# A four-layer graph network: the decoder's first expert tiles ahead of the last block's routing, joined with spare store buffers, node numbers loaded by POOL, and projection weights at the far end of memory

## The chip, the cores and the metric

The kernel runs on one core of a Trainium2 chip. The core has five engines with queues of their own: PE (TensorE, matmul), DVE (VectorE), ACT (ScalarE), POOL (GpSimd) and SP (SyncE, which only issues transfers). Sixteen DMA engines move data between HBM and the on-chip memories SBUF (128 partitions) and PSUM (where matmuls accumulate). DMA transfers are issued from the queue of an engine, here SP's, POOL's or ACT's, and that engine's instructions run in their order. The metric is the device time of one execution in microseconds (us).

## The reference, cut to what matters

Four layers, each a masked graph attention and a feed-forward part with residuals, over 2708 nodes of 256 features in fp32. The change touches the end of layer 1's feed-forward part and all of layer 2.

```python
# layer 1, feed-forward: one of eight experts for each node
H = gelu(xf @ W1 + b1)                                  # 2708 x 1024
probs = softmax(H @ Wg + bg); assign = argmax(probs)
for e in range(8):
    out = out + where(assign == e, probs[:, e] * (H @ Wd[e] + bd[e]), 0)

# layer 2, graph attention: dense over 2708 x 2708, masked by adj
e = where(adj > 0, leaky_relu((Wh @ a1)[:, None] + (Wh @ a2)[None, :]), NEG)
h_prime = softmax(e, axis=1) @ Wh

# layer 2, feed-forward: causal attention, then two of eight experts for each node
h = rmsnorm(x, ln1_w)
q, k, v = h @ wq.T, h @ wk.T, h @ wv.T                  # 4 heads of 64, 2 key/value heads, rope on q and k
y = softmax(causal(q @ k.T / 8)) @ v
x = x + y @ wo.T
flat = rmsnorm(x, ln2_w)
probs = softmax(flat @ router_w.T); tp, ti = top_k(probs, 2); tp = tp / sum(tp)
for e in range(8):
    hh = silu(flat @ w1[e].T) * (flat @ w3[e].T)        # hidden width 682
    out = out + weight_of(e) * (hh @ w2[e].T)
x = x + out
```

On the reference's inputs the eight experts of layer 2 hold 796, 754, 680, 588, 740, 790, 519 and 549 slots (node and choice), in tiles of 128: 7, 6, 6, 5, 6, 7, 5 and 5, together 47. After the first 2560 nodes they hold 759, 715, 636, 561, 700, 745, 485 and 519.

## The kernel before, in words

The 2708 nodes are 22 tiles of 128 (the last has 20 rows), the residual X stays in SBUF. The kernel is written for a framework that orders instructions by the order of the code and places all waits; `tc.issue_after(i)` pins what follows behind instruction i. Memory comes from pools that are used as stacks from either end; `side="right"` puts a pool at the far end. A pool's memory can be used only when what lay there before is free, and the framework makes the first writer wait for that.

**Layer 1, feed-forward (`top1_ffn`, L877).** In blocks of up to 512 nodes, F = gelu(x W1) is computed transposed, then turned back by PE (L960), copied to a buffer `hr` of [128, 512] (L961, ACT or DVE) and stored to DRAM as `hidden` (`store`, L950). For the last two blocks, which are stored late, `store` takes eight slots of `room`, three spare tiles that reuse other buffers (L1018–L1023); the second of them gets no room and uses the `hr` buffers, of which there are three. Meanwhile each node's slot with its expert is found and its number scattered to DRAM. `route.finish()` works out which expert each of the tiles of 128 slots belongs to. `load_first` (L1627, called at L1040) reads the node numbers of the first eight tiles on SP's queue, PE transposes them (L1045 on), and POOL gathers rows of `hidden` by them for the expert matmuls (y, L1110).

**Layer 2, graph attention (`gat_single` "g2", L1164).** A loop over column blocks i0 and, within, over 22 source tiles j (L1296 on): ACT makes e (L674), DVE masks it (L675), PE accumulates (acc, L1310). During it the experts' weights w2 are loaded (`Weights`, L1366), by 16 transfers from SP after a memset of POOL.

**Layer 2, attention (`attention`, L1691).** The pool `a_w` (L1732) holds ln1, wv, wk and wq, loaded on POOL's queue (L1735, L93) when the graph attention's memory is free, and scaled by ln1 in six DVE operations (L1739). `project` makes q, k and v of one of six column blocks of 512 nodes (the last has 148), beginning with the normed rows f (L108), their transposes (tp, L1759) and pv (L123). `attend` (L1793) goes over the key tiles: sc (L1817, PE), e = exp (L1830, ACT), masks on the diagonal (L1834), po (L1836, PE), and sums of e (L1842), of which every third goes to a second sum on POOL:

```python
                part = j % 3 == 2
```

At the end pd (L1848, PE) adds up the sums, yt is 1/pd times po (L1852, L1853). The last block does both pairs of heads at once (m = 2). `send` (L1857) is a generator: wo (wy, L123), residual, root mean square (Newton iteration, L313–L322), transposes, router logits (L1899), and `Routing.chunk` (L1468), which finds both choices by first maximum (L855–L861), their rank within the expert (L1497), and scatters the rows h with their numbers to slots of `hs` in DRAM (L1518, POOL). Block n−1's `send` and block n+1's `project` run between the key steps of block n, paced by `between`: 14 steps are counted for `send`. After the last block its own `send` runs alone, `weights.more()` loads w3 (eight transfers of 682 KB, SP, L1392).

**Layer 2, experts (`experts`, L1951).** Before it `route.finish()` (L1528) counts and assigns tiles to experts; then `owners` (L1569, what each tile holds and where its results go), `shares` (softmax weights of the two choices, and `Head`, the next layer's weights). Tiles 0 to 7 are the first tile of each expert, so their place in `hs` is known beforehand; later ones are read through a register (L1625). A tile s goes: f (fetched by SP, five buffers), PE transposes (tp) and ACT copies to ft (`front`), h = ft w1 and ft w3 (`hidden`, L1990, two halves of 682 columns), SiLU (L2003), `gate` on DVE (hh, L2007), six transposes pt (L2014), copies to ht (L2015 on DVE, L2016 on ACT), po = ht w2 (L2022), y (L2026) and `send`, the scatter of the results by POOL (L1648). `place(s)` (`where`, L1633) works out, in three DVE operations from f's last two columns, to which row each result goes. The loop pipelines two tiles, and in it `place(s + 2)` stands before `gate(s + 1)`:

```python
                        front(s + 2)
                        place(s + 2)
```

`through(0, route.usual)` does the 47 usual tiles; `others` (L1596) is a conditional body for more, entered when `further` says that there are more, which on these inputs it does not. Then `combine` reads the results back in layer 3.

## Time and profile before

| | |
|---|---|
| median of three executions | 2853.9 us (2853.67 to 2859.36) |
| profiled execution | 2853.26 us, span 2851.6 us |
| granted clock of TensorE | 0.955 |
| busy, share of the span | PE 92%, PEld 57%, DVE 51%, ACT 36%, POOL 13% |
| end of layer 1's stores to its first y | 1208 to 1227 us |
| last acc of layer 2 to the first pv | 1616.0 to 1628.6 us |
| last exp of attention to the first pt of the experts | 2102.1 to 2145.1 us |
| expert tiles, first pt to last | 2145.1 to 2531.2 us |

The page is one profiled execution. PEld is the loading of weights into PE, which overlaps matmuls. PEclk is the clock that PE was granted, as a share of full speed. A group reads: line, engine, operation, out<-in, shape, count, busy us and mean ns, idle time before it and what ended it. The chain of waits is the chain of work that ended last, followed back from the end to what released each step. A fp32 matmul makes several records.

### The profile page before, as it was taken

Reading aid. Unit: us, or ns where it says so; the run is one execution under the profiler, and the core shown is the slowest. Engines: PE = TensorE matmul, PEld = TensorE weight load, DVE = VectorE, ACT = ScalarE, POOL = GpSimd, SP = SyncE. Lnnn points to the kernel's source line nnn. Section 1 sums busy time; section 2 is a strip of 40 time slices with the busy share of each in tenths; the row PEclk is TensorE's granted clock in tenths of the full one; section 3 lists DMA queues with packets and bytes.
Section 4 is the critical chain, followed back from the end, with each engine's and each line's share of the span. In section 5 each row is a group of like instructions: output and inputs, shape, how many; then the busy total and the mean of one; then the engine's idle time right before and its main releaser. Section 6 shows DMA issues by size and latency. Waiting matters only on the chain.

```text
span 2851.6 us, 32365 instructions
## 1 busy us (share of the span) xinstructions
PE 2625.3 (92%) x11712; PEld 1616.6 (57%) x11712; DVE 1446.4 (51%) x3086; ACT 1040.0 (36%) x1639; POOL 381.5 (13%) x470
## 2 busy tenths in 40 slices
PE   5999989799999999888999899999969999969998
PEld 4667746563333444577788533333337777757885
DVE  7753348453777765422544456464653222245555
ACT  3344433224665653311543223233322221225453
POOL 1000012100000001143300123223331111110002
PEclk9999999797999999989999999899979999989999
DMA  8899210000000003753200100002031111041001
GB/s 295 288 299 326 97 65 1 3 5 1 1 1 1 1 3 115 169 176 128 85 1 1 34 23 18 16 0 94 16 117 32 30 30 34 28 137 62 1 1 40
DMA packets 107336, 197.67 MB, mean 69 GB/s; under 512 B 8831, under 2 KB 64361, under 8 KB 104341
## 3 DMA queue, kind: packets, MB, share of 16 engines
q1 hardware_dynamic: 89178, 147.89, 16.4%
q0 software_dynamic: 14624, 43.22, 4.6%
q10 hardware_dynamic: 3374, 4.46, 0.5%
q8 instruction: 98, 1.61, 0.2%
q14 instruction: 62, 0.50, 0.1%
HBM read 135.82 MB, written 59.71 MB: 69 GB/s over the span
## 4 chain that ended last, share of the span: by engine, by line
PE 74%; DVE 9%; issue 5%; DMA 5%; ACT 3%; POOL 3%; another core or an unknown queue 0%; ACTq 0%; SPq 0%; POOLq 0%; DVEq 0%
PE acc L1310 15%; PE acc L805 8%; PE acc L284 7%; PE den L816 4%; PE po L2022 4%; PE po L1836 3%; PE sc L1817 3%; PE score L273 3%; PE pv L123 3%; PE h L1990 3%; DMA f<-hs 2%; PE h L943 2%; PE po L123 2%; PE sc L1785 2%; PE pl L123 1%
## 5 line engine op out<-in xcount | busy, mean ns | idle before, releaser
L675 DVE SCALAR_TENSOR_TENSOR e<-e,mask 128x768 f32<-128x768 f32 (+2 forms) x264 | 411.3, 1573 | 310.2 <-ACT e L674 309.9
L674 ACT ACTIVATE e<-big_p,minus_one,ratio 128x768 f32<-128x768 f32 (+2 forms) x264 | 394.9, 1513 | 368.4 <-PE acc L1310 229.7
L1310 PE MATMUL acc<-V,e 128*128 128x257 f32 (+1 forms) x1936 | 433.5, 383 | 4.5 <-DVE e L675 4.4
L1310 PEld LDWEIGHTS acc<-V,e 128*128 128x128 f32 (+1 forms) x1936 | 352.3, 186 | 85.7 <-issue 32.1
L805 PE MATMUL acc<-e,V 128*64 128x512 f32 (+1 forms) x1056 | 244.3, 551 | 4.4 <-DVE e L675 4.4
L1990 PE MATMUL h<-w,ft 128*128 (+1 forms) x752 | 233.5, 453 | 0.5 <-ACT ft L1972 0.5
L284 PE MATMUL acc<-F,e 128*128 128x257 f32 x968 | 226.3, 384 | 3.1 <-DVE e L281 2.7
L284 PEld LDWEIGHTS acc<-F,e 128*128 128x128 f32 x968 | 173.4, 185 | 67.1 <-DVE e L281 28.5
L805 PEld LDWEIGHTS acc<-e,V 128*64 128x64 f32 x1056 | 107.5, 137 | 163.8 <-issue 131.2
L1817 PE MATMUL sc<-qt,kt 64*128 64x512 f32 (+5 forms) x568 | 177.2, 576 | 4.1 <-ACT e L1830 2.4
L1830 ACT ACTIVATE e<-sc 128x1024 f32<-128x1024 f32 (+3 forms) x120 | 99.6, 859 | 188.8 <-PE sc L1817 169.4
L1990 PEld LDWEIGHTS h<-w,ft 128*128 128x128 f32 x752 | 136.1, 191 | 56.7 <-issue 1.4
L281 DVE TENSOR_TENSOR e<-e,mask 128x512 f32<-128x512 f32 (+2 forms) x132 | 80.4, 625 | 150.3 <-ACT e L275 148.7
L1842 DVE TENSOR_TENSOR sum<-sum,e 128x1024 f32<-128x1024 f32 (+4 forms) x88 | 100.1, 1138 | 77.2 <-ACT e L1830 70.0
L275 ACT ACTIVATE e<-score 128x512 f32<-128x512 f32 (+2 forms) x132 | 69.7, 544 | 179.1 <-PE score L273 152.5
L2022 PE MATMUL po<-w,ht 114*128 (+1 forms) x564 | 129.5, 379 | 0.9 <-DVE ht L2015 0.9
L1836 PE MATMUL po<-e,V 128*64 128x512 f32 (+3 forms) x480 | 111.7, 547 | 16.8 <-ACT e L1830 8.7
L816 PE MATMUL den<-e,low 128*3 128x512 f32 (+1 forms) x1056 | 123.8, 542 | 0.3 <-DVE e L675 0.3
L2022 PEld LDWEIGHTS po<-w,ht 114*128 114x128 f32 x564 | 106.7, 189 | 22.6 <-DVE ht L2015 8.2
L1638 DVE TENSOR_SCALAR second<-f,down 128x1 f32<-128x1 f32 x47 | 9.9, 213 | 213.2 <-DMA f<-hs 213.2
L1817 PEld LDWEIGHTS sc<-qt,kt 64*128 64x128 f32 (+1 forms) x568 | 60.8, 191 | 94.1 <-issue 78.0
L273 PE MATMUL score<-QK 128*128 128x512 f32 (+2 forms) x264 | 112.1, 555 | 1.2 <-ACT e L275 0.7
(618 smaller groups left out, 3510.9 us busy)
## 6 DMA issues: line engine op xcount, KB each, us to landing
row<-in_adj SPq DMA_DIRECT2D x21, 1354.0 KB
raw<-in_adjT SPq DMA_DIRECT2D x35, 768.0 KB
hs<-zero SPq DMA_DIRECT2D x8, 2838.0 KB
hidden<-hr SPq DMA_DIRECT2D x34, 256.0 KB
wd<-in_f_wd SPq DMA_DIRECT2D x8, 1024.0 KB
kept<-mask SPq DMA_DIRECT2D x21, 338.5 KB
mask<-kept SPq DMA_DIRECT2D x21, 338.5 KB
f<-hs SPq DMA_DIRECT2D x47, 129.0 KB
```

The lines of the kernel that those rows point to most:

```text
L123: self.nc.tensor.matmul(out, lhsT[:, c, :], rhs[:, c, :], start=first and c == 0, stop=last and c == n - 1)
L273: nc.tensor.matmul(ps[:r, :iw], QK[:, 0, span(j)], QK[:, 1, i0 : i0 + iw], start=True, stop=True)
L284: nc.tensor.matmul(acc[k][:ri], e[:r, k * P : k * P + ri], F[:r, j, :], start=j == 0, stop=j == NT - 1)
L674: nc.scalar.activation(v, big_p[:, i], AF.Relu, bias=net.minus_one, scale=ratio)
L675: return nc.vector.scalar_tensor_tensor(v, v, 1.0, net.mask[:, j, i], ALU.add, ALU.mult)
L805: made = nc.tensor.matmul(acc[n][half, :iw], V[:, j, h, :], e[:, k, i0 : i0 + iw], start=j == 0, stop=j == NT - 1)
L816: made = nc.tensor.matmul(den[g : g + Q, :iw], low[:, j, h, Q - 1 - q : 2 * Q - 1 - q], e[:, k, i0 : i0 + iw], start=False, stop=j == NT - ...
L1310: nc.tensor.matmul(acc[k][:ri], e[:, k * P : k * P + ri], V[:, j, :], start=j == 0, stop=j == NT - 1)
L1817: nc.tensor.matmul(by_pairs(ps[:r, g])[:, :, o:], kt[b, span(j)], qt[b, :, o:iw], start=True, stop=True)
L1836: nc.tensor.matmul(by_pairs(po[b])[:, :, o:], V[:r, j, g, :], by_pairs(e[:r, g])[:, :, o:], start=j == 0, stop=j == last,)
L1990: last = nc.tensor.matmul(halves[s, n][:, q, :HALF], fts[s][:, c, :], weights.w13[n][:, es[s], c, q * HALF : (q + 1) * HALF], start=c == 0 ...
L2022: last = nc.tensor.matmul(po, ht[:KP, k, :], w2[:KP, es[s], k, :], start=k == 0, stop=k == KC - 1)
```

## The change

Four things are changed.

1. `store` takes its buffers from `room` for both late blocks, and `room` has a fourth spare tile (the buffers of `w1`, four more [128, 512]).
2. `load_first` issues from POOL's queue in place of SP's.
3. `a_w` lies at the far end of memory; in the changed program POOL's queue has the loads of ln1, wv, wk and wq directly after the memset of w2, early in the graph attention. The six scalings are pinned behind that loop's masked e of j = 3 in the first column block.
4. In attention's last block all sums are DVE's, the results lie in a tile `yl` of their own, and 24 steps are counted for block n−1's `send`. After it `route.cut` works out, from the counts of five blocks, where the results of the first eight tiles go (128 slots, or as many as the expert holds so far). Attention calls `mixture`, which loads the SiLU table by a small operation, fetches eight tiles at once (three from ACT's queue, five from POOL's, eight buffers instead of five), and runs the tiles with `beside`, a generator with the last block's `send`, `finish`, `owners` and `Head`, of which a step is taken at two places before the first pt and at three in every tile after it, until tile 4 takes what is left. `shares` comes after the last tile's gate, without `Head`. `place(s + 2)` stands behind `gate(s + 1)`. Since a tile was taken before all nodes were routed, `finish` sets `further` high if an expert lacked slots then and got them later; the conditional body then does the first eight tiles again.

The diff, cut to its core:

```diff
-                        hr = room.pop(0) if room else rp.tile([P, 512], F32, name="hr", bufs=3)
+                        hr = room.pop(0) if late else rp.tile([P, 512], F32, name="hr", bufs=3)
...
+            spare.append(work.tile([P, 2 * HID // 512, 512], F32, name="spare", tag="w1", bufs=1))
             room = [t[:, k, :] for t in spare for k in range(t.shape[1])]
             for k in kept:
                 store(*k, True, room)
-                room = ()
...
+                if i0 == 0 and j == 3:
+                    net.looped = masked
...
     with ExitStack() as inner:
         weights = Weights(net, inner)
-        attention(net, route, ln2, router, weights)
-        route.finish()
-        prep = ctx.enter_context(tc.tile_pool(name="g3prep", bufs=1))
-        work = inner.enter_context(tc.tile_pool(name="d_wt", bufs=1))
         heads = []
-        def shares():
+        def shares(work):
             route.weights(work)
             total = work.tile([P, NT], F32, name="total")
...
             nc.vector.reciprocal(total, total)
             for c in range(2):
                 nc.vector.tensor_tensor(route.weight[:, c, :], route.weight[:, c, :], total, ALU.mult)
+        def head(work):
             heads.append(Head(net, prep, work, "g3", False))
-        experts(net, route, weights, shares)
+        def mixture(after, rest):
+            experts(net, route, weights, after, rest, head, shares)
+        attention(net, route, ln2, router, weights, mixture)
     return heads[0], route
...
+    def cut(self, psum, tag):
+        nc, E, pool, key = self.net.nc, self.E, self.pool, self.key
+        ps = psum.tile([P, E], F32, name="so_many", tag=tag)
+        nc.tensor.matmul(ps, self.net.ones, self.count, start=True, stop=True)
+        self.had = pool.tile([P, E], F32, name=f"{key}had")
+        nc.vector.tensor_scalar(self.had, ps, float(P), None, ALU.min)
+        own, taken, spare = self.cuts = [pool.tile([P, E], F32, name=f"{key}cut{k}") for k in range(3)]
+        nc.vector.tensor_scalar(own, self.part, self.at, None, ALU.add)
+        nc.vector.tensor_scalar(taken, self.had, self.at, None, ALU.is_gt)
+        nc.vector.tensor_tensor(spare, taken, self.place[:, :E], ALU.mult)
+        nc.vector.tensor_tensor(spare, self.place[:, :E], spare, ALU.subtract)
+    def finish(self, psum=None, tag="total"):
         net, nc, tc, E, S = self.net, self.net.nc, self.net.tc, self.E, self.tiles
         past, total, whole, sums = self.past, self.total, self.whole, self.sums
         n = sums[:, 0, 4:]
-        with tc.tile_pool(name=f"{self.key}finp", bufs=1, space=PSUM) as psum:
-            ps = psum.tile([P, E], F32, name="total")
+        with nullcontext(psum) if psum else tc.tile_pool(name=f"{self.key}finp", bufs=1, space=PSUM) as psum:
+            ps = psum.tile([P, E], F32, name="total", tag=tag)
             nc.tensor.matmul(ps, net.ones, self.count, start=True, stop=True)
             nc.vector.tensor_scalar(n, ps, 1.0, -1.0, ALU.max, ALU.add)
             nc.vector.tensor_copy(total, ps)
...
         nc.vector.scalar_tensor_tensor(self.row, self.ex[:1], float(CAP), row[:1], ALU.mult, ALU.add)
         nc.vector.tensor_copy(self.expert, self.ex[:1])
         nc.vector.tensor_copy(self.further, sums[:1, 3, 4 + E - 1 :])
+        if self.cuts:
...
+            missing = self.pool.tile([1, 1 + E], F32, name=f"{self.key}missing")
+            nc.vector.tensor_scalar(missing[:, 1:], total[:1], float(P), None, ALU.min)
+            nc.vector.tensor_tensor(missing[:, 1:], missing[:, 1:], self.had[:1], ALU.subtract)
+            nc.vector.tensor_reduce(missing[:, :1], missing[:, 1:], AX.X, ALU.add)
+            nc.vector.scalar_tensor_tensor(
+                self.further, missing[:, :1], float(S), sums[:1, 3, 4 + E - 1 :], ALU.mult, ALU.add
+            )
...
-        more = self.net.nc.values_load(self.further, min_val=0, max_val=self.tiles)
+        more = self.net.nc.values_load(self.further, min_val=0, max_val=self.tiles * (1 + self.E * P))
...
-            self.loaded = sync.dma_start(f, self.hs[s * CAP : s * CAP + P, :])
+            self.loaded = (engine or sync).dma_start(f, self.hs[s * CAP : s * CAP + P, :])
             return
-        with nullcontext() if s == self.usual else self.net.tc.issue_after(self.loaded.ins):
+        with nullcontext() if s in (self.E, self.usual) else self.net.tc.issue_after(self.loaded.ins):
...
-        self.loaded = self.net.nc.sync.dma_start(
-            f, self.hs.rearrange("(e c) d -> e (c d)", e=self.E)[:, :P]
-        )
-    def where(self, work, s, f):
+        self.net.nc.gpsimd.dma_start(f, self.hs.rearrange("(e c) d -> e (c d)", e=self.E)[:, :P])
+    def where(self, work, s, f, cut=False):
         nc = self.net.nc
+        own, taken, spare = self.cuts if cut else (self.own, self.taken, self.spare)
...
+        wp = proj.enter_context(tc.tile_pool(name="a_w", bufs=1, side="right"))
         pp = proj.enter_context(tc.tile_pool(name="a_p", bufs=2))
         ln1 = wp.tile([P, 2], F32, name="ln1")
         nc.gpsimd.dma_start(ln1, a["d_ln1"].rearrange("(c p) -> p c", p=P))
         wv, wk, wq = (net.load_weight(wp, a[f"d_w{n}T"], f"w{n}") for n in "vkq")
-        for w in (wv, wk, wq):
-            for c in range(2):
-                nc.vector.tensor_scalar(w[:, c, :], w[:, c, :], ln1[:, c : c + 1], None, ALU.mult)
+        with tc.issue_after(net.looped.ins):
+            for w in (wv, wk, wq):
+                for c in range(2):
+                    nc.vector.tensor_scalar(w[:, c, :], w[:, c, :], ln1[:, c : c + 1], None, ALU.mult)
...
+            if m == 2:
+                results[n] = one.tile([P, 2, iw], F32, name="yl")
...
+                part = j % 3 == 2 and m == 1
...
+                waiting.append(send(n - 1, rp, aux))
+                steps[1] += 14 if n + 1 < len(cols) else 24
             for p in range(len(queries[n])):
-                attend(n, p)
+                exp = attend(n, p)
             for rest in waiting:
                 for _ in rest:
                     pass
             waiting.clear()
+        route.cut(aux, "aux")
         core.close()
         weights.more()
-        for _ in send(len(cols) - 1):
-            pass
+        mixture(exp, lambda *work: send(len(cols) - 1, *work))
...
-        def fetch(s):
-            fs[s] = work.tile([P, D + 2], F32, name="f", bufs=5)
-            route.load(s, fs[s])
+        def fetch(s, engine=None):
+            fs[s] = work.tile([P, D + 2], F32, name="f", bufs=E)
+            route.load(s, fs[s], engine)
         def front(s):
             f = fs[s]
...
             ft = fts[s] = work.tile([P, 2, P], F32, name="ft", bufs=3)
             nc.scalar.copy(ft, ps)
-        def place(s):
-            tos[s] = route.where(work, s, fs.pop(s))
+        def place(s, cut=False):
+            tos[s] = route.where(work, s, fs.pop(s), cut)
...
-        def through(s0, s1):
-            for s in range(s0, min(s0 + 4, s1)):
-                fetch(s)
+        def through(s0, s1, beside=iter(()), cut=False):
+            def step():
+                with tc.issue_after(last.ins):
+                    next(beside, None)
+            for s in range(s0, min(s0 + (E if cut else 4), s1)):
+                fetch(s, (nc.scalar if s < 3 else nc.gpsimd) if cut else None)
             front(s0)
             number(s0, nullcontext())
             number(s0 + 1, nullcontext())
             for q in range(2):
                 last = hidden(s0, 0, q)
             silu(s0)
+            step()
             front(s0 + 1)
             for q in range(2):
                 last = hidden(s0, 1, q)
             gate(s0)
-            if s0 == 0:
-                route.owners()
-            place(s0)
-            place(s0 + 1)
-            if s0 == 0:
-                shares()
+            step()
+            with tc.issue_after(gates[-1].ins):
+                place(s0, cut)
+                place(s0 + 1, cut)
             for s in range(s0, s1):
                 if s + 1 == s1:
                     results(s, transposes(s))
...
                     ht = transposes(s)
                 last = hidden(s + 1, 0, 1)
                 silu(s + 1)
+                step()
                 with tc.issue_after(last.ins):
                     last = results(s, ht)
-                if s + 4 < s1:
+                step()
+                if s == 4:
+                    for _ in beside:
+                        pass
...
+                if s + 4 < s1 and (s + 4 >= E or not cut):
                     fetch(s + 4)
                 if s + 2 < s1:
                     with tc.issue_after(last.ins):
                         front(s + 2)
-                        place(s + 2)
...
                 gate(s + 1)
-        through(0, route.usual)
+                step()
+                if s + 2 < s1:
+                    with tc.issue_after(gates[-1].ins):
+                        place(s + 2, cut and s + 2 < E)
+        def routing():
+            pool = ctx.enter_context(ExitStack())
+            yield from rest(pool.enter_context(tc.tile_pool(name="e_r", bufs=1)), pf, "tp")
+            with tc.issue_after(copied[-1].ins):
+                route.finish(pf, "tp")
+            yield
+            yield
+            with tc.issue_after(copied[-1].ins):
+                route.owners()
+            yield
+            pool.close()
+            room = ctx.enter_context(tc.tile_pool(name="e_room", bufs=1))
+            with tc.issue_after(copied[-1].ins), tc.issue_after(route.sent.ins):
+                head(room)
+            rooms.append(room)
+        rooms, silus, gates, copied = [], [], [], []
+        with tc.issue_after(after.ins):
+            nc.scalar.activation(work.tile([P, 1], F32, name="warm", bufs=1), net.ln_eps, AF.Silu)
+        through(0, route.usual, routing(), True)
+        with tc.issue_after(silus[-1].ins), tc.issue_after(gates[-1].ins):
+            shares(rooms[0])
         with route.others():
+            through(0, E)
             through(route.usual, route.tiles)
```

## The prediction

> **What bounds the kernel now.** I read the page first, then the chain of waits over the places that the diff touches, then windows and waits of the expert tiles. The page gives the frame: the profiled execution took 2853.26 us with a span of 2851.6, 1.7 around it, and stands 0.6 below the median of 2853.9; all sums below are against 2853.3.
>
> ```profile
> PE 2625.3 (92%) x11712; PEld 1616.6 (57%) x11712; DVE 1446.4 (51%) x3086; ACT 1040.0 (36%) x1639; POOL 381.5 (13%) x470
> PE 74%; DVE 9%; issue 5%; DMA 5%; ACT 3%; POOL 3%; another core or an unknown queue 0%; ACTq 0%; SPq 0%; POOLq 0%; DVEq 0%
> L1638 DVE TENSOR_SCALAR second<-f,down 128x1 f32<-128x1 f32 x47 | 9.9, 213 | 213.2 <-DMA f<-hs 213.2
> ```
>
> TensorE bounds it nearly everywhere, so a gain must come out of the 8% in which PE is idle or at a low clock. Windows (columns: PE, PEld, DVE, ACT, POOL busy, clock, DMA share, GB/s) around the last attention block and in the expert tiles:
>
> ```profile
> 2108.00:2113.00 5.00, 2.40 (x7) 1.25 (x8) 2.47 (x2) 0.00 (x0) 2.87 (x3) 0.50 0.59 133
> 2113.00:2125.00 12.00, 6.32 (x24) 3.51 (x23) 7.70 (x41) 1.42 (x5) 1.56 (x2) 0.50 1.03 396
> 2125.00:2145.00 20.00, 9.32 (x25) 5.46 (x25) 15.29 (x78) 3.01 (x5) 5.53 (x8) 0.62 0.36 117
> 2145.00:2195.00 50.00, 49.95 (x224) 36.90 (x225) 13.15 (x33) 10.56 (x24) 6.63 (x13) 1.00 0.11 33
> 2195.00:2480.00 285.00, 277.92 (x1211) 201.75 (x1210) 70.72 (x166) 59.72 (x136) 36.15 (x68) 1.00 0.10 31
> ```
>
> From 2108 to 2145 PE is half idle and at half clock; from 2145 to 2195 it is full; afterwards it loses 7 us in 285. The chain of waits (start, duration, what) says who holds the first stretch:
>
> ```profile
> 2106.33 1.45 POOL sum L1842
> ...
> 2107.83 1.28 PE pd L1848 x4
> 2109.13 2.02 DVE yt L1852
> ...
> 2111.68 3.92 PE wy L123 x8
> ...
> 2133.73 4.60 DMA av<-in_g_a
> ...
> 2145.05 0.87 PE pt L2014 x6
> ```
>
> First a POOL sum queued behind scatters of the fifth block, then routing on DVE, then the load of the next layer's head. The other two places, in the chain at layer 1's end and before attention:
>
> ```profile
> 1208.73 5.47 DMA hidden<-hr
> 1218.89 4.29 DMA hr<-hidden,number
> 1618.75 7.02 DMA wq<-in_d_wqT
> ```
>
> **What the Trainium skill says.** "TensorE: Matmul & The Clock Gate", Part 1 (the HAM clock gate): the clock halves after an idle window of about 3.4 us and returns after about 3.4 us of work. The trace agrees: 0.50 in 2108–2125, and eight h rows take 4.78 us at 2135.64 where twelve take 3.60 at 2232.62. The same page, on engine queue depths, calls DVE "strict FIFO". It shows here: place's first operation waits up to 5.4 us for f, and the gate (L2007) behind it ends late. "DMA: Bandwidth & Descriptors", section "Issuing engines are not separate DMA queues": loads from SP, ACT or POOL share the same 16 engines; w3 alone holds them at 378–428 GB/s from 2110 to 2125. So f on other queues escapes SP's order, not w3's traffic.
>
> **Part by part.**
>
> *Spare store tile and numbers by POOL (L950, L1018, L1627).* The last 20-row copy waits for an hr buffer until 1213.6 and the last store is issued at 1214.2. With four more [128,512] buffers that copy needs none freed. But load_first waits on all stores in either version, and those transfers saturate DMA until 1213. What goes is the tail: the late small store (about 1) and SP's sequencing (last store at 1214.2, numbers issued at 1215.99, landed 1217.3; POOL's fetch at 1218.89 follows, a POOL issue costing 0.6–0.7 as for the scatters' neighbours). Unknown, bounded by 0 (landing of the stores rules) and −4; I take −2.0. POOL has nothing else queued there but the fetches, which need these numbers.
>
> *Projection weights at the far end (L1732).* Now ln, wv, wk, wq are issued at 1616.59–1618.75 after layer 2's memory falls free; wq's 7.02 us and DVE's scalings (wq 1625.80, 0.49) precede f (L108) at 1626.84 and PE tp at 1627.22. After it, the loads are issued about 1376 by POOL and the six scalings sit behind the masked e of j=3. DVE, without scalings before f, can do f at about 1621 (its norms at 1618–1620 wait for nothing else), so pv, 1628.58 before, starts near 1623.0: −5.6, bounds −3 (rope's load, issued 1617.5, or DVE's norms come next) and −8. The scalings (2×0.29+2×0.34+2×0.49, with overlap about 2.3 us) move to 1404, where DVE is busy 5.27 of 12 us and three e buffers run ahead: 0; without that cover up to 2.3. The 0.8 MB of loads join w2's, which run at 135–210 GB/s from 1374 to 1408, far below the 400 of the w3 stretch; late, they would stop DVE and then PE at 1404 for a few us. Four POOL issues at 0.72 delay nothing but POOL's X additions (1404.79).
>
> *Sums by DVE in the last block (L1842).* Seven POOL additions (1.46 each) become DVE's, 0.77 each: 5.4 us more on a DVE that is busy 29.9 of 52 us from 2050 to 2102: hidden. pd then needs only the group already done at 2103.34–2104.06; PE's second group ended at 2109.1: −5.0. Bounds −3 (DVE backlog or the denser pacing, 24 steps for 14) and −5.5. The fifth block's eight POOL scatters (2100.13 to 2111.5, 1.28 apart) matter more than before, since ACT's table load and every first f now wait for them. With 24 steps their rows are ready some eight key tiles before the end instead of one; a key tile takes about 2.1 us (22 from 2056 to 2103), so they run about 2086–2096 and are no cover lost. Were they as late as before, f0 would be 10 late.
>
> *First tiles ahead.* Path after: pd ends 2104.1. The SiLU table load (1.28 us, as measured at 2135.60; "ScalarE: Activation LUTs", section "What ACT_TABLE_LOAD costs", has the same 1.28) is done before f. ACT issues f0 at about 2105.0–2105.8. The loop's f takes 2.1 us from issue (2232.81) to use (2234.95); w3's first 682 KB, issued 2104.3, need about 1.7 at 400 GB/s plus some 2 of landing. Both are there near 2108. tp 0.66 and ft copy 0.4 give h at 2109.1, at half clock after 3.5 idle us: 4.78, to 2113.9. One wy (four of its eight rows' work) 1.0, tp of f1 0.3, second half 2.3, wy 1.0, first half of tile 1 1.15: pt at 2119.6. Before, pt was at 2145.05: −25.45, of which 5.0 are the sums', 20.4 this part's. The head (DMA 4.60 and eight DVE operations at 0.33–0.42) and finish/owners (2125–2132) leave this path. If f0 or w3 lands 2–8 late, so much is lost.
>
> *Routing beside tiles 0–4.* What PE did in its idle time now takes tile time: transposes of h 0.6, router 1.0, ranks 0.6, totals 0.3: +2.5 (wy is counted). It shares the one tp PSUM buffer with the loop's transposes, each evicted by DVE or ACT, and every DVE step stands in line before a gate or an ht copy. DVE has 13.15 busy of 50 us there, so the 25–30 us of routing fit in five 8.15 us periods; bounds 0 and +10, taken +1.5. Together +4.0. The head's four a-operations wait for av, 4.6 late at worst; POOL issues it behind the results' sends, some two tiles earlier: 0, up to 4.6.
>
> *Place after the gate, f buffers 5 to 8 (L2014 in the waits of PE).* Starts of DVE's ht copy stand 8.15 apart over tiles 0–6 and the last six (2145.95 to 2194.89 in six steps, 2483.48 to 2524.21 in five), and 8.49 between 2194.89 and 2483.48, 34 steps: 34×0.336=11.4. The waits of PE put 8.7 of it on the gate:
>
> ```profile
> PE pt L2014 <- DVE hh L2007: 8.7, 32, 1.0
> ```
>
> place (three operations, ending 0.08 before the gate begins at 2235.59) moves behind it, 0.56 us under pt's 0.87, and f lands a tile or more earlier. −11.0; bounds −6 (some f still late, then holding the ht copy) and −11.4.
>
> *Shares at the end.* Three short DVE operations (0.25, 0.34, 0.34) and one exp table load after the last gate: +0.3; ahead of the 9 us of sending and reloading results (2536.48, 3.48; 2540.03, 5.16) they would be free. The larger conditional body is jumped over: its count stays zero since on the reference's inputs every expert holds at least 485 slots of the first 2560 nodes, so none lacks 128. Taken as 0.
>
> Sum: −2.0 −5.6 −5.0 −20.4 +4.0 −11.0 +0.3 = −39.7, so 2853.3 becomes about 2814 in the profiled execution and in the median.
>
> **Rivals.** (a) *The start is bound by transfers*: f0 and w3 land 6–10 late, since scatters, w3 and f share the engines (1.03 share in 2113–2125) and PE stays at half clock longer: +8, 2822. For it: 396 GB/s already reached there; against it: the first w3 piece alone is needed. (b) *DVE in line becomes the bound in tiles 0–5*: routing's chains (2116–2123 is one unbroken row of 0.17–0.2 us operations) or av hold gates and ht copies by 2–3 us in each of five tiles: +12, 2826. Against: 74% of DVE is free there. (c) *The change doesn't do what it says in the loop*: f's load is still issued late, and the wait only moves from gate to ht copy: 2825. (d) *Slower*: the joined steps leave PE gaps long enough to keep the half clock through tiles 0–4. Each full tile at half clock costs 8.15 more, five of them 41: 2855. It decides from 39.7/8.15=4.9 tiles. For it: exactly this clock in 2108–2143; against: between steps there are 4.6 us of h and 2.6 of po without a break.
>
> **How the numbers follow.** The forecast's case (2806–2820) has 0.62, (a) 0.12, (b) 0.11, (c) 0.08, (d) 0.03 and more gain than the middle (all favourable ends, near 2803) 0.04. A remaining 0.02 sits at no change or a little slower by causes unseen. Range 2806–2829. Within 0.2% (5.7 us) is what measurement cannot tell from no change: faster 0.95, same 0.02, slower 0.03.
>
> **What would show it.** Right: pd at most 1 us after the last po; pt of tile 0 near 2120 minus what came earlier (about 2112 on the changed clock); ht copies 8.15 apart beyond tile 6, and no PE wait of pt for the gate; first fetch of numbers' rows 2 earlier, pv 5–6 earlier; PEclk 0.5 for under 10 us around the last block. Wrong: DVE as releaser of PE in tiles 0–5, periods over 9.5 there, f<-hs before an ht copy, or a stop of DVE at the scalings of layer 2.

## The result, and the profile after

The changed kernel took 2809.31 us in the median of its first four executions (2806.95 to 2812.34), the kernel before 2854.31; the ratio is 0.9834, 95% interval 0.9819 to 0.9849. Four more executions in a later series, told of below, gave a ratio of 0.9886 (0.9865 to 0.9908). By these two ratios the change makes the kernel faster by 1.1 to 1.7%. Single executions spread: fifty of the kernel before went from 2842.88 to 2862.88. The last section looks for the reason.

The profiled execution took 2806.95 us with a span of 2805.2, 46.4 less than before. The page's busy line and the shares of its chain:

```profile
PE 2603.2 (93%) x11710; PEld 1611.2 (57%) x11710; DVE 1454.0 (52%) x3102; ACT 1040.9 (37%) x1641; POOL 377.2 (13%) x470
PE 77%; DVE 8%; issue 5%; DMA 4%; ACT 3%; POOL 2%; SPq 0%; ACTq 0%; POOLq 0%; DVEq 0%
```

PE has nearly the same matmuls (11710 records for 11712), is busy for 22.1 us less, and idle for 24.3 less. Less of its work falls to half clock: in these two profiles PEclk is 0.5 for 256 us before and for 198 after. The chain's PE share rises from 74 to 77%, and f<-hs, 2% before, is gone from its list. To see where the time went, marks that both kernels pass are better than shares: starts of the first y, of the first and end of the last acc in layer 2, of the first pv, of the eleven reciprocals of attention (one for each block and pair, one for the last block), of the expert tiles' DVE copies to ht, and the end. Us between marks:

| from, to | before | after | difference |
|---|---|---|---|
| start, first y of layer 1 | 1226.99 | 1226.77 | −0.2 |
| first y, last acc of layer 2 | 389.04 | 389.49 | +0.5 |
| last acc, first pv | 12.55 | 6.14 | −6.4 |
| first pv, 6th reciprocal | 201.08 | 199.85 | −1.2 |
| 6th, 7th reciprocal | 63.17 | 57.09 | −6.1 |
| 7th, 10th reciprocal | 163.48 | 163.96 | +0.5 |
| 10th, last reciprocal | 52.82 | 45.85 | −7.0 |
| last reciprocal, ht of tile 0 | 36.82 | 13.91 | −22.9 |
| ht of tile 0, ht of tile 7 | 57.38 | 65.65 | +8.3 |
| ht of tile 7, ht of the last tile | 328.80 | 317.90 | −10.9 |
| ht of the last tile, end | 319.42 | 318.63 | −0.8 |

The rows add up to the 46.4, within the rounding of the spans. Not every row is the change's: between profiles of versions that leave a stretch alone, the first row goes from 1224.65 to 1231.31, the second from 388.2 to 391.5, the last from 318.6 to 320.7, and the one from the 6th to the 7th reciprocal from 57.1 to 65.0. Windows of the changed kernel at the start of the experts and in their tiles (columns as in the prediction):

```profile
2089.00:2092.00 3.00, 1.29 (x6) 0.78 (x4) 2.96 (x7) 1.39 (x3) 2.75 (x5) 0.52 0.78 180
2092.00:2102.00 10.00, 10.00 (x30) 6.09 (x31) 3.29 (x10) 2.13 (x6) 1.37 (x2) 0.80 1.01 384
2102.00:2152.00 50.00, 45.40 (x204) 33.22 (x203) 26.07 (x112) 9.09 (x21) 10.69 (x17) 0.97 0.27 92
2200.00:2480.00 280.00, 280.00 (x1238) 205.76 (x1238) 73.46 (x175) 60.25 (x138) 36.52 (x68) 1.00 0.10 30
```

A half idle PE at half clock lasts some 7 us instead of 37, while transfers, w3 among them, run at 384 GB/s; from 2200 to 2480 PE is busy in 280 of 280. Of the 4.6 idle us in 2102–2152, 4.4 have one cause, which the chain there shows (start, duration, what), and the waits of PE name:

```profile
2135.11 0.75 POOL g3w L1145
2135.86 3.94 DMA av<-in_g_a
...
2140.02 0.42 DVE a1t L657
...
2142.76 0.61 DVE ht L2056
2143.36 0.04 issue
2143.41 4.54 PE po L2063 x12
```

```profile
PE po L2063 <- DVE ht L2056: 4.4, 1, 4.4
```

The head's load of av is issued by POOL behind a send of results and lands at 2139.8. DVE had stood still for it for 2.5 us, with tile 4's ht copy behind; then the head's eight operations, 2.7 together, still go ahead of that copy. The po after it is slow (4.54 for 2.6), at half clock.

### The profile page after: what moved, and what is told of

Same layout as the page of the kernel before. It is cut to its first block, busy times and chain, and to the rows that moved or that the text cites. A ratio compares the mean times of both kernels' runs of the same rounds, so it can differ in the third digit from the quotient of the medians.

```text
span 2805.2 us, 32369 instructions
## 1 busy us (share of the span) xinstructions
PE 2603.2 (93%) x11710; PEld 1611.2 (57%) x11710; DVE 1454.0 (52%) x3102; ACT 1040.9 (37%) x1641; POOL 377.2 (13%) x470
## 4 chain that ended last, share of the span: by engine, by line
PE 77%; DVE 8%; issue 5%; DMA 4%; ACT 3%; POOL 2%; SPq 0%; ACTq 0%; POOLq 0%; DVEq 0%
PE acc L1311 15%; PE acc L805 8%; PE acc L284 7%; PE h L2031 7%; PE den L816 4%; PE po L2063 4%; PE po L1872 4%; PE score L273 3%; PE sc L1852 3%; PE pv L123 3%; PE h L943 2%; PE sc L1818 2%; PE po L123 2%; DMA dys<-y,to 2%; PE pl L123 1%
## 5 line engine op out<-in xcount | busy, mean ns | idle before, releaser
L1852 PE MATMUL sc<-qt,kt 64*128 64x512 f32 (+5 forms) x568 | 170.1, 566 | 4.1 <-ACT e L1866 2.4
L2048 DVE TENSOR_TENSOR hh<-hh,h 128x682 f32<-128x682 f32 x47 | 40.7, 865 | 247.5 <-PE h L2031 247.5
L1866 ACT ACTIVATE e<-sc 128x1024 f32<-128x1024 f32 (+4 forms) x121 | 100.2, 857 | 183.1 <-PE sc L1852 167.8
L1878 DVE TENSOR_TENSOR sum<-sum,e 128x1024 f32<-128x1024 f32 (+5 forms) x95 | 104.7, 1102 | 74.5 <-ACT e L1866 71.2
L1872 PE MATMUL po<-e,V 128*64 128x512 f32 (+4 forms) x484 | 112.3, 542 | 17.5 <-DVE e L1870 9.0
```

Of the source, the lines that this page charges most:

```text
L1852: nc.tensor.matmul(by_pairs(ps[:r, g])[:, :, o:], kt[b, span(j)], qt[b, :, o:iw], start=True, stop=True)
L1872: nc.tensor.matmul(by_pairs(po[b])[:, :, o:], V[:r, j, g, :], by_pairs(e[:r, g])[:, :, o:], start=j == 0, stop=j == last,)
```

## Experiments

All ratios are to the kernel before, on the same chip.

**Stores and numbers alone.** The kernel before with parts 1 and 2:

```diff
-                        hr = room.pop(0) if room else rp.tile([P, 512], F32, name="hr", bufs=3)
+                        hr = room.pop(0) if late else rp.tile([P, 512], F32, name="hr", bufs=3)
+            spare.append(work.tile([P, 2 * HID // 512, 512], F32, name="spare", tag="w1", bufs=1))
-        self.loaded = self.net.nc.sync.dma_start(
+        self.net.nc.gpsimd.dma_start(f, self.hs.rearrange("(e c) d -> e (c d)", e=self.E)[:, :P])
```

> The kernel before with the spare store tile and the node numbers issued by POOL, nothing else. Prediction: the first y of layer 1, at 1227.2 before, comes 2 us earlier, and the kernel is 2 us faster. Rival, from the trace of the changed kernel: the stores fill the DMA engines until about 1213.8 and the numbers wait for the last of them in either version, so the first y stays within 0.5 us of 1227.2 and the time does not change (0, at most 1).

Measured: ratio 1.0007 (0.9992 to 1.0022); first y at 1225.90, 1.1 earlier than in the one profile of before, where profiles of versions that leave this part alone have 1224.65 to 1231.31. The part is worth nothing that can be told. The changed kernel's chain shows where the gain went. The stores still end it at 1213.86, SP's issuing stands in it until 1216.68, the first gather of rows is issued at 1217.98 for 1218.89 before, and the gathered rows then take longer (5.68 for 4.29). Why they do was not looked into.

```profile
1198.36 6.42 DMA hidden<-spare
1204.85 9.01 DMA hidden<-spare
1216.72 0.39 DMA rowed<-fnodes
1219.29 5.68 DMA hr<-hidden,number
```

**Weights alone.** The kernel before with part 3:

```diff
+                if i0 == 0 and j == 3:
+                    net.looped = masked
-        wp = proj.enter_context(tc.tile_pool(name="a_w", bufs=1))
+        wp = proj.enter_context(tc.tile_pool(name="a_w", bufs=1, side="right"))
+        with tc.issue_after(net.looped.ins):
```

> The kernel before with the projection weights at the far end and their scalings inside the graph attention, nothing else. Prediction: the first pv, 12.5 us after the last acc before, comes 5.6 earlier. From the trace of the changed kernel, where it came 7.7 after the last acc: 4.8 earlier, and the time falls by 5 to 6.5. Rival: the acc rows of the graph attention lose what is won (the scalings or the loads hold DVE at about 1404), and the time falls by under 3.

Measured: ratio 0.9974 (0.9963 to 0.9985), 7.4 us with 4.3 to 10.6. From last acc to first pv 6.03 for 12.55, and the graph attention from its first acc to its last takes 216.56 for 216.57: the scalings in it cost nothing.

**Place behind the gate, alone.** The kernel before with

```diff
                         front(s + 2)
-                        place(s + 2)
...
                 gate(s + 1)
+                if s + 2 < s1:
+                    with tc.issue_after(gates[-1].ins):
+                        place(s + 2)
```

> The kernel before with one edit in the expert loop: place of a tile stands behind the gate of the tile before it; f keeps five buffers. Theory: the stall is place's order on DVE alone (place of a tile five ahead stood in front of the gate and waited for an f just issued), so the ht copies stand 8.15 apart over all tiles and the time falls by 11 to 11.5. Rival: with five buffers f still lands late, place then holds the ht copy, and the time falls by under 6; the eight buffers are needed as well.

Measured: ratio 0.9944 (0.9921 to 0.9967). From the ht copy of tile 7 to the last it takes 317.93 for 328.80, 10.9 less. All gaps between copies to ht are 8.15 or 8.16 but the last, 7.94. In the waits of DVE from 2205 to 2500, f<-hs, 5.4 us at a time before, has gone, and DVE waits for matmuls:

```profile
DVE hh L2007 <- PE h L1990: 202.9, 36, 5.6
DVE ht L2015 <- PE pt L2014: 12.4, 37, 0.3
```

Five buffers are enough. 34 times 0.336 are 11.4; the ratio's 16.0 has an interval of 9.4 to 22.5 and doesn't contradict it. The profile is of the slowest of the seven executions (2852.04), which lost its time ahead of the experts: its first y comes 4.3 later, and from the first pv to the 7th reciprocal it takes 6.4 more.

**Eight buffers, alone.** The kernel before with `bufs=E` for f and eight fetches at the start:

```diff
-            fs[s] = work.tile([P, D + 2], F32, name="f", bufs=5)
+            fs[s] = work.tile([P, D + 2], F32, name="f", bufs=E)
-            for s in range(s0, min(s0 + 4, s1)):
+            for s in range(s0, min(s0 + (E if s0 == 0 else 4), s1)):
-                if s + 4 < s1:
+                if s + 4 < s1 and (s + 4 >= E or s0 > 0):
```

> The kernel before with eight buffers for f and eight tiles fetched at the start, all by SP; place is not moved. Theory that only place's order counts: f is issued eight tiles ahead instead of five, place goes with it and still stands in front of a gate behind an f that was just issued, so the ht copies stay 8.49 apart and the time changes by 0 (at most 2). Rival, that f came too late: 8.15 apart, and the time falls by 11.

Measured: ratio 1.0042 (1.0029 to 1.0054), 12 us slower. Between tiles 6 and 39 most copies stand 8.74 to 8.95 apart, every few tiles 9.4 to 10.1. Waits of DVE, then of PE, from 2200 to 2485:

```profile
DVE second L1638 <- DMA f<-hs: 162.5, 30, 5.8
...
DVE to L1642 <- DMA dys<-y,to: 25.5, 29, 6.2
...
PE pt L2014 <- DVE hh L2007: 22.3, 32, 1.8
```

Both theories missed the sign. f comes three tiles earlier, and place goes with it: DVE's order is not the code's here, and place of the tile just loaded stands directly ahead of the gate. So it is in the kernel before, at the gate of tile 11:

```profile
2234.95 0.21 DVE L1638 TENSOR_SCALAR second<-f,down 128x1 f32<-128x1 f32 x1 [5.41 <-DMA f<-hs]
2235.20 0.27 DVE L1641 TENSOR_SCALAR second<-second,f,dhas 128x1 f32<-128x1 f32 x1
2235.51 0.16 DVE L1642 TENSOR_TENSOR to<-second,dspare 128x1 int32<-128x1 f32 x1
2235.59 0.87 DVE L2007 TENSOR_TENSOR hh<-hh,h 128x682 f32<-128x682 f32 x1
```

These are the 18th set of place's operations, that of tile 17, five ahead of tile 12, whose rows PE has just transposed. With eight buffers the gate of tile 12 has the 22nd set ahead of it, that of tile 21, eight ahead of tile 13. Eight ahead it needs one of the eight `to` tiles back from a result that is only just being sent, so a second wait (for dys, 2.42 us from POOL's issue) joins the first. Earlier data with the order unmended is a loss.

**Sums alone, and sums with the pace.** The kernel before with all sums of the last block on DVE, and then with 24 steps as well:

```diff
-                part = j % 3 == 2
+                part = j % 3 == 2 and m == 1
```

> The kernel before with all sums of attention's last block on DVE, 14 steps as before. Prediction: pd no longer waits for a POOL sum behind the scatters; from the fifth block's last reciprocal to the last block's, 52.8 before, 47.8 (5 less), and the rest of the kernel as before. Rival: DVE, with seven additions of 0.77 more, now ends last, and under 3 is won.

> As the run with the sums alone, and 24 steps counted for the send of the fifth block. If the 7.0 that the changed kernel wins in this stretch is the sums' alone, both runs show 45.8 from reciprocal to reciprocal. If the faster pace adds to it (POOL free of scatters at the end, DVE's chain of routing not at the end), the run with 14 steps shows 47.8 and this one 45.8.

Measured: 0.9987 (0.9972 to 1.0001), which does not exclude no change, and 0.9980 (0.9967 to 0.9993), 5.7 us with 2.0 to 9.4. The marks tell more. From the 10th reciprocal to the last 48.00 and 46.12, 52.82 before. So 4.8 is the sums' and 1.9 the pace's. And with 14 steps 0.4 of the gain is lost again behind the reciprocal, though that stretch differs by as much between profiles. There h of the last block waits for its buffers, which the late scatters still read, as the chain shows.

```profile
2103.76 6.43 DMA hs<-h,dto
2110.19 0.04 issue
2110.23 0.64 DVE h L1875
```

From the 10th reciprocal to tile 0's ht copy it is 85.26 and 82.80, for 89.64: 4.4 and 6.8.

**Routing ahead of the first tile.** The changed kernel with the joining undone:

```diff
-            yield from rest(pool.enter_context(tc.tile_pool(name="e_r", bufs=1)), pf, "tp")
+            for _ in rest(pool.enter_context(tc.tile_pool(name="e_r", bufs=1)), pf, "tp"):
+                pass
+            route.finish(pf, "tp")
+            route.owners()
...
+            for _ in range(6):
+                yield
...
+        first = routing()
+        next(first)
-        through(0, route.usual, routing(), True)
+        through(0, route.usual, first, True)
```

> The changed kernel with the last block's send, finish and owners ahead of the first tile, in one piece (the head still beside tiles 1 and 2, everything else as changed). Theory: the gain of the first tiles is the cover of routing by matmuls. From the last reciprocal to tile 0's ht copy 13.9 becomes about 31 to 33 (36.8 before, less the head's wait of some 4 to 5), tiles 0 to 6 go back to 8.15 to 9 each, so the kernel is 10 to 14 slower than the changed one. Rival: the early fetch and the SiLU table are what won, then it is within 4 of it.

Measured: ratio 0.9937 (0.9912 to 0.9962), against 0.9834 and 0.9886 of the changed kernel: 15 to 29 us slower than it by the points, from different series, and so more than the 10 to 14 that were expected. From the last reciprocal to tile 0's ht copy 35.78 (36.82 before), to tile 7's 99.34, where the changed kernel has 79.56 and the kernel before 94.20. The joining wins 19.8 between these marks. The early fetch and the SiLU table by themselves win 1.0 at most, as far as tile 0's copy. My 31 to 33 was too low, since taking the head out of the start saved nothing that shows: with the head in it, the run with place alone has 35.70. In the kernel before, PE is busy with tile 0's h until 2144.08 and the gate begins at 2144.14, so the wait for av lay under h. Placed beside tiles 1 and 2, the head costs its 4.9 and 1.6 (gaps 13.04 and 9.73) all the same.

**The head's operations later.** The changed kernel with the eight operations taken out of tile 4; they go, two at a time, behind the ht copies of tiles 6 to 9, and the loads stay:

```diff
+                if cut and s >= 6 and folds:
+                    with tc.issue_after(copied[-1].ins):
+                        next(folds[0], None)
```

> The changed kernel with the eight DVE operations of the next layer's head taken out of tile 4 and put, two at a time, behind the ht copies of tiles 6 to 9; its two loads stay where they are. Theory: DVE stood still for the load of av (3.9 from issue) ahead of tile 4's ht copy, 4.4 of PE's time and a half clock after it. The gaps of ht copies 12.83 and 9.73 become about 8.5 and 8.2, and the time falls by 5.5 to 6.5 against the changed kernel. Rival: finish and owners hold the same copy, and under 2 is won.

Measured: ratio 0.9830 (0.9811 to 0.9848), 2805.06 in the median of four. The gaps behind tiles 3 and 4, 12.83 and 9.73 in the changed kernel, are 8.03 and 8.16, 6.4 us less, and the gaps with the operations in them are 8.16. The whole time doesn't tell the gain: 0.9830 stands beside 0.9834 and 0.9886 of the changed kernel, from three series. The operations in their new place:

```profile
2158.54 0.69 DVE L2071 COPY ht<-pt 114x512 f32<-114x512 f32 x1 [0.34 <-PE pt L2070]
2159.15 0.41 DVE L1154 TENSOR_TENSOR a1t<-g3w,av 128x256 f32<-128x256 f32 x1
2159.60 0.42 DVE L1157 TENSOR_REDUCE g3a<-a1t 128x1 f32<-128x256 f32 x1
2166.70 0.69 DVE L2071 COPY ht<-pt 114x512 f32<-114x512 f32 x1 [0.34 <-PE pt L2070]
```

**The changed kernel again, and three more edits.**

> The changed kernel once more, beside the others on one chip, for more executions. All theories: 2806 to 2812 in the median. Its spread tells whether the 6.1 us that its first profile won between the sixth and the seventh reciprocal (57.1 for 63.2) are the change's: the theory is that they are not, that every version falls on either side, by where the clock's drop after a pause of PE falls; then this profile may show 57.1 or 63 to 65 there and nothing else moves.

Measured: 2817.72 in the median (2814.37 to 2822.00), ratio 0.9886 (0.9865 to 0.9908): above the 2806 to 2812 that was expected. Its profile shows 63.18 from the 6th to the 7th reciprocal; the first profile's 57.09 was no effect of the change. Among the versions that leave these blocks alone, the eight buffers show 57.09 too, the stores 63.20, the weights 63.19, the place 64.95, the sums 64.72. The other marks repeat: 13.93 from the last reciprocal to tile 0's ht copy, 65.85 from there to tile 7's.

Fill for PE, with the head late:

```diff
+        def fill(times, after):
+            ps = aux.tile([P, P], F32, name="fill", tag="aux")
+            with tc.issue_after(after.ins):
+                for _ in range(times):
+                    after = nc.tensor.matmul(ps, net.ones, net.ident, start=True, stop=True)
...
+                if m == 2 and j == last:
+                    fill(6, score)
...
-        route.cut(aux, "aux")
+        fill(5, route.cut(aux, "aux"))
```

> The changed kernel with the head's operations behind tiles 6 to 9, and with eleven matmuls of no use (128x128, 0.27 us each): six behind the last score, five behind the count, where PE waits for exp, mask and the first f. Theory: tile 0's eight h rows take 4.48 only because PE's clock halves while it waits; filled, they take 2.4 and tile 0's ht copy comes 11.9 after the last reciprocal instead of 13.9, 2 us won. Rival: w3's first piece or f0 would then be late, or the fill is too short for the clock, and nothing is won (0 to 1 lost).

Measured: ratio 0.9868 (0.9843 to 0.9894). From the last reciprocal to tile 0's ht copy 16.38 for 13.92 with the head late alone, 2.5 worse. The second fill shares a PSUM buffer with a tile that DVE reads only after the reciprocal, so it came late, and the first expert matmuls behind it still ran at half clock:

```profile
2098.25 1.38 PE L1846 MATMUL fill<-ident,ones 128*128 128x128 f32 x10 [1.79 <-DVE dhad L1557]
...
2100.56 3.78 PE L2055 MATMUL h<-w,ft 128*128 128x341 f32 x6 [0.52 <-ACT ft L2037]
```

Whether a fill at the right place wins the 2 us stays open.

Sums of the last four key steps on DVE in every block, with the head late; then this and the fill together:

```diff
-                part = j % 3 == 2 and m == 1
+                part = j % 3 == 2 and m == 1 and j + 4 <= last
```

> The changed kernel with the head's operations behind tiles 6 to 9, and in all blocks of attention the last four key steps' sums on DVE instead of POOL. Theory: pd's waits for a POOL sum (0.9 to 1.4, 3.4 and 2.35 at the ends of blocks 3 to 5) go, 6 to 7 us, and with them the pause after which the clock halves: between the sixth and seventh reciprocal 57 or less in every execution, up to 3 more in the mean. Rival: DVE, which then has two additions of 1.14 more at each end, is late itself, and under 3 is won.

> All three edits (head late, fill, tail sums by DVE) on the changed kernel. If they add up: 6 by the head, 2 by the fill and 6 to 9 by the sums, so 14 to 17 below the changed kernel, near 2794. If the fill's gain is not there, 2796.

Measured: ratio 0.9752 (0.9736 to 0.9769), 2781.23 in the median of five (2778.50 to 2783.35), and with the fill 0.9744 (0.9726 to 0.9762), 2777.98. In the whole time the fill makes no difference that shows; from the last reciprocal to tile 0's ht copy it loses 2.1 (16.37 for 14.29). The sums' edit wins much more than the 6 to 9 of its theory: from the 5th to the 10th reciprocal 245.71, where the version with the head late alone has 271.44. Both are faster than the changed kernel (2817.72 on the same chip) and, by 2.5%, than the kernel before.

## Why the prediction was right, and where its steps were off

The forecast was 2814 for the changed kernel; the two series of executions have medians of 2809.3 and 2817.7. Step by step, by the marks of the table:

- **Spare store tile and numbers by POOL**, −2.0 forecast: 0. The step that failed is "what goes is the tail". Only a part of it went: the first gather is issued 0.9 earlier, with 2.8 of SP's issuing still between the stores and the numbers, and the rows gathered take 1.4 longer, which no term held.
- **Projection weights**, −5.6 forecast: −6.4, and −6.5 in the run of this part alone. The mechanism is as written; f begins at 1620.1 where 1621 was assumed, and the scalings cost nothing at their new place.
- **Sums by DVE**, −5.0 forecast: 4.8 for the sums alone as far as the reciprocal, 7.0 with the pace. The denser pace had been entered only as a danger. It is worth 1.9 there.
- **First tiles ahead**, −20.4 forecast: −22.9. f0 is in use 2.2 after its issue, nearly as assumed (2088.60 to 2090.8 for 2.1), but ACT issues it while the table still loads, at 0.2 after pd's beginning and not 1 to 2 after its end. The half clock came as assumed, with 4.48 for eight rows against 4.78, but by another pause: the clock drops at 2089.1, when PE had waited 1.46 and 0.19 and was busy for 1.8 of the last 3.4 us, ahead of the idle time that the working had counted.
- **Routing beside tiles 0–4**, +4.0 forecast: +8.3, the largest miss. PE's own extra work is 0.4, 0.7 and 1.1 in the gaps behind tiles 0 to 2, 2.3 together, where 2.5 was written down. The rest, 6.2 in the two gaps behind tiles 3 and 4, is the head's, whose wait for av the working had bounded at 4.6 and taken at 0, "POOL issues it behind the results' sends, some two tiles earlier". This is the step that failed. The head's loads and operations come together, and DVE reaches the first operation 2.5 before av lands; the eight operations themselves, 2.7, then stand ahead of the ht copy; and PE stood long enough to lose its clock. No term held the last two. The run with the operations later gives the 6.4 back.
- **Place behind the gate**, −11.0 forecast: −10.9. The explanation was incomplete: it was place of the tile just loaded that stood in front of the gate, further ahead than the code's `s + 2`. The eight buffers, named as half of the remedy, do nothing for it; alone they lose 12.
- **Shares at the end**, +0.3 forecast: −0.8 for the whole stretch behind the last copy. This tells nothing, since the two profiles of the changed kernel differ by 3.0 there (318.6 and 321.6).

The sum −39.7 was met by some −40, the marks without the stretch from the 6th to the 7th reciprocal, which moves by 6 to 8 us on its own. That it came so near is luck in part. Two errors cancelled: 4.3 too small a cost at the tiles, 4.5 too small a gain in sums and start. Rival (b), DVE's line holding the first tiles, described the mechanism that did occur, in one tile and not in five. With it two of the signs named for being wrong appeared, DVE as releaser of PE and periods over 9.5 (12.83 and 9.73). Of (d) one window of 3.4 us at half clock appeared, at tile 4; (a) and (c) did not occur. The chances given to the cases add up to 1.02, a slip in the working.

## What to carry to other kernels

When an in-order engine waits in a loop, ask first what stands in its line: moving a small operation behind the one that others wait for won 11 us by itself, while fetching the data earlier let the same operation run further ahead and lost 12. Work moved under a covered loop brings its own waits along; split a load from its first use, or the use stops the loop. And where executions of one program differ by more than the effect looked for, compare stretches between marks, and add up the time at half clock in each.

## What the runs showed of the hardware

The spread of single executions goes with TensorE's clock: over fifty executions of the kernel before, time and mean granted clock have a correlation of −0.80. A part of it lies in the attention blocks. In twelve profiles of versions that leave these blocks alone, the stretch from the 6th to the 7th reciprocal takes 57.1 us in the two with no time at half clock in it, 63.2 in the five with some 13.6 us at half clock, 64.7 in four with 17.1 and 65.0 in one with 17.4. What leads to that is seen in windows around the 6th reciprocal, of the kernel before and then of the changed kernel (the clock is the third figure from the end):

```profile
1812.47:1815.89 3.42, 1.49 (x6) 0.27 (x5) 3.39 (x9) 0.35 (x1) 2.34 (x1) 1.00 0.01 2
1815.89:1843.19 27.30, 25.93 (x54) 7.92 (x54) 8.60 (x15) 4.09 (x6) 8.97 (x9) 0.50 0.11 39
```

```profile
1805.79:1809.20 3.41, 1.67 (x7) 0.45 (x6) 3.37 (x9) 0.53 (x1) 2.35 (x1) 1.00 0.01 2
1809.20:1819.44 10.24, 9.60 (x26) 3.66 (x26) 2.97 (x10) 0.87 (x2) 7.35 (x8) 0.50 0.22 79
```

In both the clock halves within a pause of PE of 2.12 us, when PE had been busy for 1.5 to 1.7 of the last 3.4. Only the moment of its return differs, after 27.3 us and after 10.2. "TensorE: Matmul & The Clock Gate", Part 1, has an idle window of about 3.4 us for the drop and about 3.4 us of work for the return. Here the pause was shorter, and the return took longer although PE was busy for 25.93 of the 27.30 us; the measurement decides. The length of the unit does show: all 317 stretches at half clock that ended within the fourteen profiles last 3.41 us or a multiple of it, up to eleven times. So 10.2 are three windows and 27.3 are eight. What in a window decides on the return is not shown by these runs.

What makes the pause is seen in the timeline of the kernel before (start, duration, engine, line, operation):

```profile
1812.88 2.34 POOL L1842 TENSOR_TENSOR sum<-sum,e 128x1024 f32<-128x1024 f32 x1 [8.20 <-DVE e L1834]
...
1812.94 2.43 DVE L1504 TENSOR_TENSOR dat<-drank,done 128x32 f32<-128x32 f32 x2
1815.30 0.29 DVE L1505 TENSOR_REDUCE dslot<-dat 128x4 f32<-128x32 f32 x2
1815.52 0.17 DVE L1509 COPY dtag<-dslot 128x4 f32<-128x4 f32 x1
1815.60 0.42 DVE L1834 TENSOR_TENSOR e<-e,upper 128x256 f32<-128x256 f32 x1
...
1816.07 1.55 PE L1836 MATMUL po<-e,V 128*64 128x384 f32 x4 [2.12 <-DVE e L1834]
```

The first of the two DVE multiplications of 128x32, 0.18 us in the median of the ten of its line, takes 2.33 us here and ends when a POOL addition that began 0.06 before it has ended. "SBUF — State Buffer", section "SBUF: two separate sides", says that DVE and GpSimd take turns on a shared pair of ports, each holding it for a whole instruction; the two spans here agree with that. Behind the multiplication waits a mask, behind the mask PE. With POOL's sums of the last four key steps taken away, the two multiplications take 0.28 together, PE has no pause there, and the clock holds in the whole stretch of that version; its timeline, and then its windows:

```profile
1807.40 0.28 DVE L1526 TENSOR_TENSOR dat<-drank,done 128x32 f32<-128x32 f32 x2
```

```profile
1760.00:1830.00 70.00, 67.90 (x275) 24.91 (x274) 43.11 (x98) 25.79 (x37) 16.89 (x15) 1.00 0.05 18
1830.00:1900.00 70.00, 66.67 (x238) 22.33 (x236) 42.20 (x80) 21.50 (x30) 18.84 (x12) 1.00 0.00 1
```

Its five executions lie within 4.9 us of each other, where in that series nine of the kernel before lie within 13.3 and four of the changed kernel within 7.7. Of its 26 us from the 5th to the 10th reciprocal, the clock can have at most some 18, by this estimate: the version with the head late alone is at half clock for 36.2 us in that stretch, this one never, and what takes 36.2 at half clock takes 18.1 at full. How the rest divides between the end of pd's waits (0.9, 3.4 and 2.35 at three block ends) and the ports was not separated.
